# Where the output transposes find their PSUM bank, and when the sums of the heads' weights may start, in a two-layer graph-attention kernel

## The chip, the cores and the metric

One core of one Trainium2 chip. The metric is the device time of one execution in microseconds (us). Most executions agree within 0.3%. Faster or slower asks for 2%. A ratio is the mean time of one kernel's runs over the mean time of the other's runs of the same rounds, so it is not quite the ratio of the medians that are quoted beside it.

## The reference, cut to what matters

x is 128 graphs of 64 nodes with 512 features, all fp32. The layer is a norm, four attention heads, one more attention over the four heads' outputs, and a feed-forward with a residual and a second norm:

```python
h = relu(layernorm(x))
h = elu(gat_heads(h, adj, W_heads, a_heads))      # 4 heads, 512 -> 512 each
out = elu(gat_heads(h, adj, W_out, a_out))        # 2048 -> 512
y = relu(out @ w1 + b1) @ w2 + b2 + out
x + layernorm(y) * gamma + beta
```

## The kernel before

The 8192 rows are 64 tiles of 128, taken in 16 groups of four. Every large product is done with seven block products instead of eight (Strassen's way), so sums of weight blocks are formed once at the start by GpSimd and written to DRAM. TensorE works on one group's heads and output projection while the feed-forward of the group before and the attention of the group after are mixed in.

PSUM has eight banks here: a ring of six, tag "mm", and two auxiliary ones.

```python
ps = ctx.enter_context(tc.tile_pool(name="ps", bufs=6, space=bass.MemoryType.PSUM))

def bank(name):
    return ps.tile([P, 2, T], FP, tag="mm", name=name)

def aux(shape, name):
    return ps.tile(shape, FP, tag="aux", name=name, bufs=2)
```

Accumulators of the products (g1, g5, g6 of each unit) come from the ring. The attention of a tile takes two auxiliary banks for its first half and two of the ring for its second. ScalarE copies one bank of each pair out, VectorE the other:

```python
def task(j):                       # attend1, one tile
    ...
        if half == 1:
            banks = [bank(f"pz{nm}_{t}_{b}") for b in range(NB)]
        else:
            banks = [aux([P, 2, T], f"pz{nm}_{t}_{b}") for b in range(NB)]
        # ... eight matmuls for the two banks
    for nm, banks in done:
        for b in range(NB):
            ...
            if b == 0:
                nc.scalar.copy(dst, srcv)
            else:
                nc.vector.tensor_copy(dst, srcv)
```

For tiles 2 and 3 of a group the first half is "S1" (called pzS and zS in the profile), for tiles 0 and 1 it is "11" (pz, z). The feed-forward of the group before begins with four output transposes, one after each of these tasks, into an auxiliary bank as well:

```python
def transpose_out(j):
    ...
    pt = aux([P, KC, P], f"pto{g}_{j}")
    for k in range(KC):
        nc.tensor.transpose(pt[:, k, :], o[:, j, ts(k, P)], ident)
    nc.scalar.copy(OT[j // 2][:, :, ts(j % 2, P)], pt)
```

At the start, GpSimd does two things: a small power and a product for each tile's norm (n1rs, n1nb), which ScalarE's norm waits for, and the sums of weights. A tie keeps some sums behind the last tile's n1nb:

```python
def weight_sums(m, after=None):
    ...
    first = nc.gpsimd.tensor_tensor(s[0][:, 0], b12, b11, ALU.subtract)
    if after is not None:
        tc.add_manual_dep(first.ins, after.ins.name, ...)
    nc.gpsimd.tensor_tensor(s[0][:, 1], b22, s[0][:, 0], ALU.subtract)
    nc.gpsimd.tensor_tensor(s[1][:, 0], b22, b12, ALU.subtract)
    nc.gpsimd.tensor_tensor(s[1][:, 1], b21, s[0][:, 1], ALU.subtract)
    ...
for m in range(H):
    weight_sums(m, LAST["nb"] if m else None)
```

The names in the lines below: hn is the norm of a tile of x, pth and hT its transpose in PSUM and in SBUF. The start folds the weights of each head with its attention vector into wa: for heads 0, 1 and 3 VectorE does it (jk, out of the weights pw and of pab, the vector spread over all partitions by TensorE); for the third head, number 2, TensorE does it (pwt is the transposed weights, wT ScalarE's copy of them, aT the vectors, pwa the product). project_f (pf) multiplies hT by wa; L, U and R are made of pf; s1pe holds the first scores, R times L; s1e and s1A are steps of their softmax, s1pt its transpose. Then pz is attention times hn. g_a, g_b, g_c and g_d are accumulators of the heads' product, of the output projection (project2) and of the feed-forward's two products; zs_z holds sums of z for them. o is the layer's output, pto its transpose.

## Time and profile before

| | before |
|---|---|
| time, median of 3 runs | 2352.25 us (2352.14 to 2352.45) |
| span of the profiled run | 2349.7 us |
| TensorE busy, idle | 2281.3 us, 68.4 us |
| idle before output transposes | 26.3 us in 26 waits |
| first attention matmul (pz) | 54.16 us |

TensorE is the bound, so the idle 68.4 us are what a change of order can win; 26.3 of them repeat from group to group and most of the others lie in the first 54 us. The lines are in the prediction. In lines of single instructions the columns are start, duration, engine and line of the kernel, operation, output and inputs, and in square brackets the engine's idle time before it and what ended that.

### The profile page before, as it was taken

The page shows a single profiled execution, that of the slowest core. Times are in us where ns is not written, and L with a number is a line of the kernel's source. Part 1 is how long each engine was busy: PE and PEld are TensorE (multiplying, and loading weights), DVE is VectorE, ACT ScalarE, POOL GpSimd, SP SyncE. Part 2 cuts the span into 40 slices and gives each one's busy share as a digit, 9 for nine tenths or more (in the row PEclk, how much of TensorE's full clock was granted, in tenths as well). Part 3 has the DMA queues.
Part 4 walks back from the last instruction along what each step waited for, and adds up shares of the span by engine and source line. Part 5 has one row for each costly group of instructions (what it writes and reads, how often), then busy time and mean ns, then how long its engine had stood idle before and what let it go on. Part 6 is the DMA issues. An engine that isn't in the chain of part 4 may idle for free. (4 is left out here: it accounts for less than half of the span.)

```text
span 2349.7 us, 33387 instructions
## 1 busy us (share of the span) xinstructions
PE 2281.3 (97%) x11933; PEld 1921.8 (82%) x11933; DVE 1271.2 (54%) x2210; ACT 907.0 (39%) x1623; POOL 1031.2 (44%) x917
## 2 busy tenths in 40 slices
PE   6999999999999999999999999999999999999997
PEld 4878887888878888787888878888788887888885
DVE  5635465555646556464554655555465554744527
ACT  2534425253352533425244251533525344251512
POOL 5664444425344353443524444253443535533334
PEclk9999999999999999999999999999999999999999
DMA  8555464554645445464454645545454454645543
GB/s 287 158 183 193 129 182 132 156 160 131 182 127 173 134 143 178 127 181 129 145 173 129 182 132 156 160 130 180 129 172 136 142 178 124 181 123 158 169 148 104
DMA packets 259571, 366.40 MB, mean 156 GB/s; under 512 B 24232, under 2 KB 147144, under 8 KB 259408
## 3 DMA queue, kind: packets, MB, share of 16 engines
q1 hardware_dynamic: 252784, 343.31, 47.8%
q0 software_dynamic: 4512, 16.78, 1.9%
q10 hardware_dynamic: 2112, 4.19, 0.5%
q8 instruction: 96, 1.57, 0.3%
q14 instruction: 67, 0.55, 0.1%
HBM read 336.92 MB, written 27.26 MB: 155 GB/s over the span
## 5 line engine op out<-in xcount | busy, mean ns | idle before, releaser
L322 PE MATMUL g_b<-w,h 128*128 128x256 f32 x2560 | 592.5, 379 | 0.0
L322 PEld LDWEIGHTS g_b<-w,h 128*128 128x128 f32 x2560 | 481.4, 190 | 63.6 <-issue 0.9
L307 PE MATMUL g_a<-z,w 128*128 128x256 f32 x1520 | 360.9, 380 | 0.8 <-DVE g_a L597 0.7
L307 PE MATMUL g_a<-zs_z,w 128*128 128x256 f32 x1504 | 350.9, 381 | 0.0
L307 PEld LDWEIGHTS g_a<-zs_z,w 128*128 128x128 f32 x1504 | 282.1, 190 | 60.8 <-issue 24.3
L307 PEld LDWEIGHTS g_a<-z,w 128*128 128x128 f32 x1520 | 287.3, 190 | 45.0 <-DVE g_a L597 6.1
L601 POOL TENSOR_TENSOR hS<-hS,h 128x512 f32<-128x512 f32 x64 | 83.2, 1301 | 354.8 <-DVE hS L565 354.8
L322 PE MATMUL g_b<-w,hS 128*128 128x256 f32 x1024 | 238.5, 379 | 0.0
L563 ACT ACTIVATE exc<-g_a 128x512 f32<-128x512 f32 x256 | 152.1, 594 | 179.3 <-DVE g_a L597 106.0
L565 DVE SCALAR_TENSOR_TENSOR h<-exc,g_a 128x512 f32<-128x512 f32 x192 | 131.7, 686 | 156.0 <-ACT exc L564 156.0
L322 PEld LDWEIGHTS g_b<-w,hS 128*128 128x128 f32 x1024 | 192.1, 190 | 25.8 <-issue 1.0
L564 ACT ACTIVATE exc<-exc 128x512 f32<-128x512 f32 x256 | 161.5, 631 | 7.0
L631 POOL TENSOR_TENSOR h<-h,h 128x512 f32<-128x512 f32 x64 | 86.8, 1364 | 135.4 <-PE g_b L322 135.4
L631 POOL TENSOR_TENSOR h<-hS,h 128x512 f32<-128x512 f32 x64 | 81.1, 1269 | 142.5 <-PE g_b L322 142.5
L332 POOL TENSOR_TENSOR zs_z<-zS,z 128x512 f32<-128x512 f32 x63 | 89.0, 1414 | 122.4 <-PE g_a L307 118.4
L481 ACT COPY at<-s1pt 128x512 f32<-128x512 f32 x64 | 34.7, 588 | 279.8 <-PE s1pt L479 279.8
L773 POOL TENSOR_TENSOR xr<-xr,bs 128x512 f32<-128x512 f32 x64 | 95.7, 1500 | 72.8 <-DMA xr<-in_x_dram 40.6
L322 PE MATMUL g_d<-w,rt 128*128 128x256 f32 x512 | 121.5, 380 | 1.7 <-DVE o L765 1.0
L307 PE MATMUL g_c<-ot,w 128*128 128x256 f32 x512 | 122.5, 382 | 0.2 <-DVE ot L735 0.2
L307 PE MATMUL g_a<-zS,w 128*128 128x256 f32 x496 | 117.2, 379 | 0.0
L655 DVE SCALAR_TENSOR_TENSOR jf<-wh,ao 128x512 f32<-128x512 f32 x128 | 98.4, 806 | 32.5 <-ACT wh L637 32.3
L333 POOL TENSOR_TENSOR zs_z<-z,zs_z 128x512 f32<-128x512 f32 x63 | 85.2, 1354 | 62.3 <-PE g_a L307 39.6
(159 smaller groups left out, 3484.9 us busy)
## 6 DMA issues: line engine op xcount, KB each, us to landing
w<-tc SPq DMA_DIRECT2D x632, 256.0 KB, 2.7
w<-in_L_gnn_W_heads_dram SPq DMA_DIRECT2D x192, 256.0 KB, 3.2
w<-in_L_gnn_W_out_dram SPq DMA_DIRECT2D x192, 256.0 KB, 2.8
w<-in_L_gnn_w_dram SPq DMA_DIRECT2D x96, 256.0 KB, 2.7
x<-in_x_dram SPq DMA_DIRECT2D x64, 256.0 KB, 4.2
xr<-in_x_dram SPq DMA_DIRECT2D x128, 128.0 KB, 2.7
out_dram<-o SPq DMA_DIRECT2D x128, 128.0 KB, 2.4
tc<-pt POOLq DMA_DIRECT2D x20, 512.0 KB, 4.5
```

The lines of the kernel that those rows point to most:

```text
L307: LAST["pe"] = nc.tensor.matmul(bk[:, o, :], w[:, k, ts(o, P)], a[:, k, :], start=start and o == 0 and k == 0, stop=k == 1, skip_group_che ...
L322: LAST["pe"] = nc.tensor.matmul(bk[:, j, :], a[:, k, ts(j, P)], w[:, k, :], start=start and k == 0 and j == 0, stop=i == len(ms) - 1 and k ...
L332: eng.tensor_tensor(s2, s1, a11, ALU.subtract)
L333: eng.tensor_tensor(s4, a12, s2, ALU.subtract)
L481: nc.scalar.copy(AT[t].rearrange("p b h n -> p (b h) n"), pt)
L563: nc.scalar.activation(ex, src, AF.Relu, scale=-1.0)
L564: nc.scalar.activation(ex, ex, AF.Exp, scale=-1.0)
L565: nc.vector.scalar_tensor_tensor(dst, ex, -1.0, src, ALU.add, ALU.max)
L601: nc.gpsimd.tensor_tensor(dst, dst, H1["22"][:, h], ALU.add)
L631: nc.gpsimd.tensor_tensor(dst[:, h], x0[:, h], x1[:, h], ALU.subtract)
L655: nc.vector.scalar_tensor_tensor(junk, WH2[g][:, j], 1.0, ao[:, c, :], ALU.mult, ALU.mult, accum_out=f[:, c, j:j + 1],)
L773: nc.gpsimd.tensor_tensor(xr, xr, bs, ALU.add)
```

## The change

Its intent is to take away the two waits: the transposes use a bank of the ring, and every sum that needs only raw weights, of every head, waits for the last tile's first norm.

```diff
-        first = nc.gpsimd.tensor_tensor(s[0][:, 0], b12, b11, ALU.subtract)
-        if after is not None:
+        free = [nc.gpsimd.tensor_tensor(s[0][:, 0], b12, b11, ALU.subtract)]
+        nc.gpsimd.tensor_tensor(s[0][:, 1], b22, s[0][:, 0], ALU.subtract)
+        free.append(nc.gpsimd.tensor_tensor(s[1][:, 0], b22, b12, ALU.subtract))
+        for ins in free if after is not None else ():
             tc.add_manual_dep(
-                first.ins, after.ins.name,
+                ins.ins, after.ins.name,
                 ...
-        nc.gpsimd.tensor_tensor(s[0][:, 1], b22, s[0][:, 0], ALU.subtract)
-        nc.gpsimd.tensor_tensor(s[1][:, 0], b22, b12, ALU.subtract)
@@
-            pt = aux([P, KC, P], f"pto{g}_{j}")
+            pt = bank(f"pto{g}_{j}").rearrange("p a b -> p (a b)").rearrange("p (k n) -> p k n", k=KC)
@@
-        weight_sums(m, LAST["nb"] if m else None)
+        weight_sums(m, LAST["nb"])
```

## The prediction

> **What bounds the kernel now.** I read the page first, then all waits of TensorE, then busy times by stretch, then the order of time in one repeat of the steady state and in the first 55 us.
>
> ```profile
> PE 2281.3 (97%) x11933; PEld 1921.8 (82%) x11933; DVE 1271.2 (54%) x2210; ACT 907.0 (39%) x1623; POOL 1031.2 (44%) x917
> PEclk9999999999999999999999999999999999999999
> ```
>
> The span is 2349.7 us (2352.25 us is the timed median), so TensorE is idle for 2349.7 - 2281.3 = 68.4 us in all. No other engine is over 54%, and the clock is granted in full. A change that leaves the arithmetic alone, as this one does, can at most win those 68.4 us (2.9%). So the list of TensorE's waits is the list of what can be won:
>
> ```profile
> PE pto L725 <- ACT zS L551: 26.3, 26, 1.9
> PE pab L158 <- DMA ar<-in_L_gnn_a_heads_dram: 8.3, 1, 8.3
> PE s1pt L479 <- DVE s1A L442: 5.4, 1, 5.4
> PE pwa L193 <- ACT wT L191: 5.2, 1, 5.2
> ```
>
> The reader sees one wait that comes 26 times, and single ones of the start. The first is the output transposes waiting for a ScalarE copy of zS, which is no input of theirs: it only reads the PSUM bank that they are to be written to. The stretches show where it repeats:
>
> ```profile
> 380.00:520.00 140.00, 138.09 (x732) 116.78 (x731) 78.17 (x134) 54.71 (x99) 61.04 (x53) 1.00 0.50 152
> 520.00:660.00 140.00, 138.09 (x733) 116.78 (x732) 76.98 (x133) 54.64 (x99) 59.32 (x52) 1.00 0.51 154
> 2060.00:2200.00 140.00, 140.00 (x689) 119.34 (x688) 66.21 (x115) 50.84 (x91) 57.28 (x46) 1.00 0.51 153
> ```
>
> The second number is TensorE's busy time in 140 us. One repeat (a group of four tiles) is about 142.4 us long and loses 1.91 us; the stretch from 2060, where no first norms are left to do, loses nothing with the same banks. Inside a repeat:
>
> ```profile
> 397.40 0.69 DVE L553 COPY z<-pz 128x512 f32<-128x512 f32 x1 [0.24 <-PE pz L539]
> 397.41 0.81 ACT L366 ACTIVATE hn<-x,n1nb,n1rs 128x512 f32<-128x512 f32 x1
> 398.13 0.57 ACT L551 COPY zS<-pzS 128x512 f32<-128x512 f32 x1
> 398.59 0.59 ACT L551 COPY z<-pz 128x512 f32<-128x512 f32 x1
> 398.75 0.42 PEld L725 LDWEIGHTS pto<-ident,o 128*128 128x128 f32 x4 [1.89 <-ACT zS L551]
> 398.75 0.66 PE L725 MATMUL pto<-ident,o 128*128 128x128 f32 x4 [1.49 <-ACT zS L551]
> ```
>
> Both auxiliary banks hold pzS; ScalarE's part of the copy stands in its queue behind the norm of a later tile (hn); the transposes start 0.05 us after that copy ends (398.13 + 0.57 = 398.70). The fourth transposes of the group lose another 0.42 us in the same way, so 1.49 + 0.42 = 1.91 us. The first two of a group follow z11's copy and show no idle TensorE.
>
> The start, on GpSimd and ScalarE:
>
> ```profile
> 18.22 1.27 POOL L219 TENSOR_TENSOR pt<-pw,pt 128x512 f32<-128x512 f32 x1
> 19.43 1.31 POOL L222 DMA_DIRECT2D tc<-pt  x2
> 20.76 2.50 POOL L218 TENSOR_TENSOR pt<-pw 128x512 f32<-128x512 f32 x2
> 23.21 0.56 POOL L356 TENSOR_TENSOR n1rs<-n1ve,mhalf 128x1 f32<-128x1 f32 x1
> ...
> 24.17 1.69 ACT L366 ACTIVATE hn<-x,n1nb,n1rs 128x512 f32<-128x512 f32 x2 [8.34 <-POOL n1nb L364]
> 25.77 0.16 ACT L170 COPY aT<-pah 128x32 f32<-128x32 f32 x1
> 25.83 1.07 ACT L191 COPY wT<-pwt 128x512 f32<-128x512 f32 x2
> ```
>
> VectorE had the variances of tiles 2 and 3 at about 15.0 us, but GpSimd took up their small power operation (n1rs) only at 23.2, behind sums of weights that are needed much later. ScalarE stands for 8.34 us, and behind it in its queue the copies wT that TensorE's pwa waits for. The existing tie covers only the first sum of heads 1 to 3; L218, whose inputs are raw weights too, slips ahead of it.
>
> **What the Trainium skill says.** "Perfetto Trace Analysis", section "Identifying the Most-Contended Engine", warns that matmul occupancy is a poor measure of headroom and takes the weight loads' busy share instead. Here that is 82%, but in the repeats both are level from stretch to stretch, so I use idle time before named instructions, not the percentages. The same page, "Optimization Strategy", says that the same gap repeating on the saturated engine can mean too little PSUM for the next tile; this trace agrees: 26 gaps of one kind. "PSUM — Partial Sum Buffer", section "Specifications (TRN2)", gives 8 banks of 512 fp32 values; the ring of six and two auxiliary ones are all, and a transposed tile (128x512 fp32) fills one, so the change can only shift load between the two pools. That page's section "Engine vs sequencer instructions" says ScalarE's, VectorE's and GpSimd's queues are strict FIFO; both chains above are an urgent instruction behind an idle one, so the trace agrees.
>
> **The change part by part.** No operation is added or removed; banks and order change.
>
> *Part A, the bank.* A ring bank must be free when the third transposes of a group come. In the repeat above that is 397.3 us. Live in the ring are then: project2's first accumulator (begun at 381.1, read again for its second product some 20 us on) and the two pz banks of this tile (copied by 399.2). The other three were last read by 393 us: the two pz banks of the tile before (copies ended at 391.9 and 392.1) and the second output transpose (its copy ended at 392.5). One goes to the transposes, one to project2's next accumulator, one is left. At the fourth transposes (about 403 us in the new time) two accumulators and two pz banks are live, and two are free. The three or four further accumulators of the feed-forward come after that, as today. So I expect no new wait, and the two auxiliary banks, with 3.5 us of other matmuls between the third transposes and the next pzS, have time to be copied. Gain: 13 groups (1 to 13, the ones that still have norms) at some 2.0 us (1.91 in twelve of them, 1.49 + 1.87 = 3.36 in the last) = 12 x 1.91 + 3.36 = 26.3 us, just the line above. VectorE, GpSimd and the weight loads are tied to TensorE's progress and have slack (54%, 44%, DMA 0.5), so I let the gain run through whole, less 1 us for small new gaps: 25 us.
>
> *Part B, the sums.* Tied behind the last n1nb, the three sums that need raw weights cannot start before about 17 us: n1rs and n1nb of tiles 2 and 3 are 2 x (0.56 + 0.26) = 1.6 us after 15.0. So hn of tile 3 ends at about 18 instead of 25.9, 8 us earlier. TensorE cannot use it all: its transposes pwt of the third head end at 19.31 + 1.97 = 21.3 anyway, held by weights' landing and by VectorE's folds. So pwa starts at 21.3 instead of 26.47: 5.2 us, and the folds, project_f and the first scores follow in a chain of fixed lengths (VectorE's last folds start after a pab matmul that stands behind pwa). If the new order of instructions also puts pab earlier, up to 8. I take 6. The sums end on GpSimd at about 17 + 16 x 1.27 + 8 x 0.57 + 2 x 0.72 = 43 us instead of 41; head 0's are needed at about 55 and the written-back ones later, so that delay is hidden. From 60 us on TensorE is the bound (59.2 of 60 us busy), so the gain is kept to the end.
>
> Sum: 2352.25 - 25 - 6 = 2321 us, 1.3% less.
>
> **The rivals.** (1) *The wait moves into the ring.* If the bank given to the transposes or to the accumulator after them is one whose reader is late, the 1.9 us come back, or more: accumulators live 20 to 40 us. For it: project2 and the feed-forward together hold six accumulators at times. Against: they come after the last transposes, and in group 15 (2230 to 2244 us) four transposes pass with no idle time. Part A would then give 0 to 10 us, time 2335 to 2346; with a new wait of 3 us in each group it would be over 2360. (2) *ScalarE, not the bank, is the limit.* Its queue delays the copy of zS whatever bank the transposes use; the next pzS, or project1 through the sums of z, would then wait instead. For it: the copy is late because of a norm. Against: 3.5 us of cover, and ScalarE is busy only 39%. It would make the gain of A about half: 2333. (3) *The start is bound elsewhere.* DMA share is 0.87 in the first 54 us, and a first norm or the third head's weights may rest on a landing; B would then be 0 to 3 us: 2324 to 2327. (4) *The start does better*, if pab of head 3 moves ahead of pwa and VectorE's folds close up (they stand idle 8.1 + 4.8 us): B near 10, time 2317.
>
> **Range and chances.** Both parts in full with the better start give 2316; A at half and B at 3 give 2336. Range 2314 to 2337. Faster by over 2% needs 47 us of the 68.4 idle, of which A and B reach at most 37: 3%. Slower by over 2% needs a new wait of over 3 us in every group and nothing won: 3%. Within 2%: 94%.
>
> **What would show it.** Right: the wait of pto for zS is gone from TensorE's list, the stretches of 140 us show 140 busy, a repeat is 140.5 us long instead of 142.4, the idle time of TensorE is near 37 us. For B: n1rs of tile 2 at about 15 us, ScalarE's wait of 8.34 us gone, project1's first pz at about 48 instead of 54.16 us. Wrong: a new line of pto, g_b or g_c waiting for a copy of z or for an accumulator's reader (rival 1), of pzS or g_a waiting for ScalarE (rival 2), or pwa still at 26 us (rival 3).

## The result, and the profile after

The changed kernel takes 2320.33 us, median of 4 runs (2317.49 to 2320.77), against 2352.35 us of before in the same rounds: 32.0 us less. The ratio is 0.9861, with a 95% interval of 0.9844 to 0.9878: the same by the 2% rule, and clearly not by chance. The order of instructions on TensorE and ScalarE is exactly that of before; only GpSimd's order and a few of VectorE's small instructions at the start differ. So nearly the whole gain is waiting that went away: TensorE's idle time fell by 29.5 us, of the 31.0 us by which the two profiled spans differ.

TensorE's waits, all engines' instructions, longest first (the columns: who waited for whom, total us, times, longest us):

```profile
PE pab L158 <- DMA ar<-in_L_gnn_a_heads_dram: 8.2, 1, 8.2
PE s1pt L479 <- DVE s1A L442: 5.4, 1, 5.4
```

The line of 26.3 us is gone, and so is pwa's 5.2 us; nothing of their size stands in their place (the third longest wait is 2.8 us). The steady stretches of 140 us are full, from 240 to 1920 us (one of them; columns as in the prediction: stretch, its length, TensorE's busy time):

```profile
380.00:520.00 140.00, 140.00 (x742) 118.58 (x740) 78.33 (x134) 56.01 (x101) 60.22 (x53) 1.00 0.49 154
```

The same place in the repeat as the prediction showed of before, now in the changed kernel:

```profile
390.66 0.66 PE L725 MATMUL pto<-ident,o 128*128 128x128 f32 x4
...
390.88 0.81 ACT L366 ACTIVATE hn<-x,n1nb,n1rs 128x512 f32<-128x512 f32 x1
...
391.59 0.57 ACT L551 COPY zS<-pzS 128x512 f32<-128x512 f32 x1
```

ScalarE's copy of zS is as late as it was (it still follows the norm hn), but the transposes now run 0.9 us before it starts instead of 0.05 us after it ends. The first output transposes of successive groups started at 386.98 and 529.40 us before (a repeat of 142.42 us) and start at 380.44 and 520.82 us now (140.38 us).

The start, on GpSimd and ScalarE, in the changed kernel:

```profile
14.45 0.55 POOL L356 TENSOR_TENSOR n1rs<-n1ve,mhalf 128x1 f32<-128x1 f32 x1 [1.41 <-ACT hn L366]
...
16.31 1.28 POOL L210 TENSOR_TENSOR pt<-pw 128x512 f32<-128x512 f32 x1
...
15.39 1.68 ACT L366 ACTIVATE hn<-x,n1nb,n1rs 128x512 f32<-128x512 f32 x2 [0.32 <-POOL n1nb L364]
...
18.67 0.58 ACT L191 COPY wT<-pwt 128x512 f32<-128x512 f32 x1 [1.52 <-PE pwt L189]
```

The norm of tile 2 is served at 14.45 us instead of 23.21, and ScalarE's copies wT start at 18.67 instead of 25.83, now behind TensorE's pwt. TensorE's pwa starts at 20.99 instead of 26.47 us. The first pz, though, is at 49.61 instead of 54.16 us: of 5.5 us at pwa only 4.55 are left there. What lies between is the one place where the trace did not go as told; two of the instructions of that chain, in the changed kernel:

```profile
38.41 1.26 POOL L211 TENSOR_TENSOR pt<-pw,pt 128x512 f32<-128x512 f32 x1
...
38.91 1.32 DVE L399 TENSOR_TENSOR R<-U,headrow 128x512 f32<-128x512 f32 x1
...
40.37 1.99 PE L413 MATMUL s1pe<-R,L 64*64 64x256 f32 x16 [2.82 <-DVE n1ve L354]
```

and in the kernel before, where GpSimd had no sums left:

```profile
45.02 0.66 DVE L399 TENSOR_TENSOR R<-U,headrow 128x512 f32<-128x512 f32 x1
...
45.82 1.09 PE L413 MATMUL s1pe<-R,L 64*64 64x256 f32 x16 [2.16 <-DVE n1ve L354]
```

R took twice as long with a sum of weights running beside it, and the 16 score matmuls that wait for it took 1.99 us instead of 1.09 after a longer idle time. The granted clock of just these two stretches shows why the matmuls were slow (columns: stretch, its length, busy time of TensorE, of its weight loads, of VectorE, ScalarE and GpSimd, granted clock, DMA share, GB/s). First the changed kernel, then the kernel before:

```profile
40.37:42.36 1.99, 1.99 (x16) 0.86 (x16) 1.11 (x2) 0.00 (x0) 1.99 (x3) 0.50 0.98 290
```

```profile
45.82:46.91 1.09, 1.09 (x16) 0.57 (x16) 1.09 (x2) 0.00 (x0) 1.09 (x3) 0.99 0.68 239
```

Each trace also records when which clock was granted. It was full at 36.89 to 40.30 us in the changed kernel and at 43.48 to 46.90 in the kernel before, with half the clock after it (to 53.95 and 57.14 us). The score matmuls of the changed kernel started 0.07 us after that stretch had ended.

### The profile page after: what moved, and what is told of

It reads as the page before. It is cut to its first block, busy times and chain, and to the rows that moved or that the text cites. A ratio compares the mean times of both kernels' runs of the same rounds, so it can differ in the third digit from the quotient of the medians.

```text
span 2318.7 us, 33446 instructions
## 1 busy us (share of the span) xinstructions
PE 2279.8 (98%) x11933; PEld 1922.7 (83%) x11933; DVE 1272.2 (55%) x2210; ACT 905.5 (39%) x1623; POOL 1029.9 (44%) x917
```

## The experiments

**The theory**: (A) the transposes waited for nothing but a bank whose reader stood late in ScalarE's queue, another bank removes that whole, and nothing takes its place; (B) the start was held by sums of weights in front of the norms in GpSimd's queue. **The rivals**: the wait moves to the ring; ScalarE is the limit whatever the bank; the start is bound by something else. Runs e1 to e4 shared one chip and the runs of before (median 2352.01 us), as did e5 to e8 (2352.32 us) and e9 to e12 (2351.82 us).

### e1: the bank alone

Edit: the change's line of `pt = bank(...)` only. The order of instructions on every engine is that of before.

> Only the bank of the output transposes is changed; the sums keep their old tie. The order of instructions on every engine is that of the kernel before. My theory (the 26.3 us of waiting for the copy of zS is all bank, and nothing takes its place): 2325 to 2327 us, no wait of pto for zS left, 140.0 us busy in each steady stretch of 140. Rival 'ScalarE's queue is the limit': under half of it, 2338 or more, with new waits of pzS or g_a for ScalarE.

Measured: 2325.43 us (2324.28 to 2325.83), 26.6 us less, ratio 0.9886 (0.9872 to 0.9899). No wait of pto for zS is left and the steady stretches are 140.00 of 140 busy. Part A is as the theory has it; the rivals of part A would have left half or none of it.

### e2: the sums alone

Edit: the change without its line of `pt = bank(...)`.

> Only the sums are tied behind the last tile's norm; the transposes keep the auxiliary bank. My theory: the start is 4.5 us shorter as in the changed kernel's trace (first pz at 49.6 instead of 54.2 us) and TensorE's 26 us of waits stay: 2347 to 2348.5 us. If part of the 31 us comes from both together, this and the run with the bank alone do not add up to 31 to 32 us.

Measured: 2348.08 us (2347.95 to 2348.65), 3.9 us less, ratio 0.9984 (0.9971 to 0.9996); TensorE's 26.4 us of waiting for zS stay. Here R took 2.33 us beside the sums, and the first pz came at 49.88 us.

### e3: the old bank, but zS copied by VectorE

```diff
-                    if b == 0:
+                    if b == 0 and nm != "S1":
                         nc.scalar.copy(dst, srcv)
```

in the kernel before, with bank and tie as they were.

> The kernel before, with the bank and the tie as they were, but VectorE copies both banks of zS, so that neither stands in ScalarE's queue behind a norm. My theory (bank held by a copy that is late in ScalarE's queue): the third transposes' 1.49 us shrink to below 0.3, and the fourth's 0.42 too or nearly, so 2328 to 2334 us. If the cause were TensorE's transposes needing more banks as such, whoever empties them: the wait stays, 2350 us or more, now put down to VectorE.

Measured: 2326.01 us (2325.63 to 2326.4), 26.0 us less, ratio 0.9889 (0.9874 to 0.9904): a somewhat larger gain than expected and nearly what the other bank gives. (The order of TensorE's instructions differs in places from that of before.) In this run's trace the norm is still in ScalarE's queue, and it does not matter:

```profile
395.60 1.29 DVE L553 COPY zS<-pzS 128x512 f32<-128x512 f32 x2 [1.09 <-PE pzS L539]
...
396.36 0.66 PE L725 MATMUL pto<-ident,o 128*128 128x128 f32 x4
396.59 0.81 ACT L366 ACTIVATE hn<-x,n1nb,n1rs 128x512 f32<-128x512 f32 x1
```

One of the two auxiliary banks was free in time, and the transposes start with no idle TensorE. So two auxiliary banks were enough, and the wait was the late reader's: a bank that is freed in time and another bank that is free are two cures of one wait.

### e4: the change once more

> The changed kernel once more, on the chip and in the rounds of the single parts. 2318 to 2321 us; the parts alone should add up to this within 1.5 us.

Measured: 2318.78 us (2317.71 to 2320.49), 33.2 us less, ratio 0.9859 (0.9846 to 0.9873). The parts alone add to 26.6 + 3.9 = 30.5 us, 2.7 us short; I had allowed 1.5, so this expectation failed. The traces show where: in the profiled run of e4 the first eight pwa matmuls took 0.95 us, in those of e2 and of the first run of the changed kernel 1.70 to 1.71 us, with the same instructions in the same order. e4's first pz came at 47.54 us, theirs at 49.88 and 49.61. So the opening itself runs in one of two paces, some 2 to 3 us apart (project_f, before anything collides, starts at 31.84 us in e4, at 34.70 in e2 and at 35.41 in the changed kernel's first run), and a median of four runs probably mixes them (2317.49 us is the lowest and 2320.77 us the highest of the eight runs of the changed kernel). The clock records tell the two apart. In e4 the full clock was granted from 19.78 to 23.19 us, over the first sixteen pwa matmuls (0.95 us for eight), and half from there to 33.43 us, where the other sixteen took 3.58 us; in e7 below, the other fast opening, full from 20.48 to 23.89. In e2 and in the changed kernel's first run the record has no entry before 35.43 and 36.89 us (the view prints 1.00 for a stretch without an entry), and all their pwa went at the pace of e4's half clock, so I take it that they ran at half. Why the full clock is granted early in some runs stays open. In what follows I compare the openings of like pace, by their traces.

### e5: head 0's sums left untied

```diff
-        weight_sums(m, LAST["nb"])
+        weight_sums(m, LAST["nb"] if m else None)
```

in the changed kernel.

> The changed kernel (transposes in the ring), but head 0's sums stay untied; for heads 1 to 3 all three sums of raw weights are tied. GpSimd then does head 0's four sums and two transfer issues before n1rs of tile 2, which I put at 19.5 us (23.2 before, 14.5 in the changed kernel). pwa at about 22.9 us (26.5 before, 21.0 changed), so 1.5 to 2.5 us slower than the changed kernel of these rounds: about 2321. If the tie of head 0 is what matters, 4 us slower (2323 or more).

Measured: 2320.91 us (2320.34 to 2321.68), ratio to before 0.9868 (0.9851 to 0.9884). The places are as expected: n1rs of tile 2 at 19.44 us, pwa at 22.71. Yet the first pz is at 50.33 us, only 0.7 us after the changed kernel's, though pwa is 1.7 later: the sums end earlier, R took 0.66 us, and the score matmuls, 1.20 us long, met the full clock for most of their time.

### e6: only the first sum of each head tied

```diff
-        for ins in free if after is not None else ():
+        for ins in free[:1] if after is not None else ():
```

in the changed kernel.

> The changed kernel, but of each head only the first sum is tied, head 0 included (the half of the tie that the kernel before lacked for head 0). The four other raw sums still slip ahead: n1rs of tile 2 at about 18 us. The transposes of the third head end at 21 us anyway, so pwa at about 21.4 and the time within 1 us of the changed kernel. If every us of GpSimd counts, 3 us slower.

Measured: 2324.35 us (2324.27 to 2324.8), ratio 0.9882 (0.9867 to 0.9896): nearly all of part B is lost (the first pz is at 53.79 us, against 54.16 before), and the expectation failed. GpSimd's queue shows why:

```profile
21.54 1.27 POOL L212 TENSOR_TENSOR pt<-pw 128x512 f32<-128x512 f32 x1 [3.96 <-DMA pw<-in_L_gnn_W_heads_dram]
22.77 0.54 POOL L356 TENSOR_TENSOR n1rs<-n1ve,mhalf 128x1 f32<-128x1 f32 x1
```

The untied sum of head 3 needs weights that landed only at 21.5 us. It is first in a queue that is served in order, so the norm stands 3.96 us behind a transfer that is none of its business. I had counted the work in front of the norm, and not its waits.

### e7: head 3's sums behind the first softmax

```diff
-    for m in range(H):
+    for m in range(3):
         weight_sums(m, LAST["nb"])
@@
     softmax_end = LAST["A"]
+    for m in range(3, H):
+        weight_sums(m, softmax_end)
```

in the changed kernel.

> The changed kernel, but head 3's sums wait for the end of the first softmax, so that GpSimd is idle beside VectorE's first scores. Theory from the runs so far: the tied sums run 2 us later while VectorE's chain runs 5.5 us earlier, they now overlap, and VectorE's instructions with two SBUF inputs (R at 1.3 to 2.3 us instead of 0.66, two of the softmax at 2 us instead of 0.69) are held up by them. Expect all of these back at 0.7 us, and 1 to 2.5 us less than the changed kernel: about 2317. Rival: their length has another cause (data not there yet); then they stay long and the time stays at 2318.5 to 2320.

Measured: 2317.04 us (2314.97 to 2319.45), ratio 0.985 (0.9836 to 0.9865). R took 0.66 us, the softmax's instructions 0.66 to 0.69, and the score matmuls 1.09 us. Its profiled run opened in the faster pace (pwa 0.97 us), so it is to be held against e4's: first pz at 44.90 instead of 47.54 us, 2.6 us. In e4 it was two of the softmax's instructions that had been long, beside the same sums:

```profile
38.36 2.09 DVE L431 SCALAR_TENSOR_TENSOR s1e<-s1e 128x512 f32<-128x512 f32 x1
...
41.21 1.97 DVE L434 TENSOR_TENSOR s1e<-s1e,s1mx 128x512 f32<-128x512 f32 x1
```

The reduction between them kept its 0.69 us, but no sum ran beside it (GpSimd was at n1rs, from 39.86 to 41.40 us), so it is no test.

### e8: pab of head 3 ahead of the third head's fold

```diff
+    ab[3] = spread_a(3)
     fold_pe(2, aT)
@@
-    fold_dve(3, spread_a(3))
+    fold_dve(3, ab[3])
```

in the changed kernel.

> The changed kernel, with the two matmuls pab of head 3 issued ahead of the third head's fold on TensorE. Tests what the prediction left as its fourth rival: the gain of the sums is limited because pab of head 3 stands behind pwa. VectorE's folds should then run without the two gaps (3.5 and 4.8 us in the changed kernel), and TensorE's pwa chain should have a third buffer for its copies. Expect the first pz 3 to 6 us earlier than in the changed kernel, time 2313 to 2317. If instead the transposes pwt, now waiting for a bank behind VectorE's first folds, set the start, no gain or a loss.

Measured: 2320.72 us (2320.18 to 2321.26), ratio 0.9866 (0.985 to 0.988): no gain. The edit did what it was for: project_f starts at 32.32 us instead of 35.41. Then comes R, here VectorE's and GpSimd's lines of the same time:

```profile
35.83 4.68 DVE L399 TENSOR_TENSOR R<-U,headrow 128x512 f32<-128x512 f32 x1
...
36.25 1.27 POOL L210 TENSOR_TENSOR pt<-pw 128x512 f32<-128x512 f32 x1
37.48 1.26 POOL L212 TENSOR_TENSOR pt<-pw 128x512 f32<-128x512 f32 x1
38.70 1.26 POOL L211 TENSOR_TENSOR pt<-pw,pt 128x512 f32<-128x512 f32 x1
```

R, 0.66 us of work, ends at 40.51 us, 0.55 us after the third of three sums in a row. The score matmuls start at 40.66 us, against 40.37 in the changed kernel: all 3 us are given back. (They also took 1.99 us, at a granted clock of 0.50.) This is the clearest sight of what also cost part B its last part.

The Trainium skill has the mechanism: "SBUF — State Buffer", section "Who interferes with whom", says that a VectorE instruction with two SBUF inputs contends with a GpSimd instruction that reads SBUF, and one with a single SBUF input does not. The traces agree: R and the two softmax instructions above, with two inputs in SBUF, went from 0.66 to as much as 4.68 us and from 0.69 to 2.09 and 1.97 us. In all six cases in the openings where such an instruction of R or of the softmax met a sum (the changed kernel, e2, e4 twice, e6, e8), it ended 0.55 or 0.56 us after the last sum that it met. The statistics of x, with one input, took 1.28 us for two beside sums (changed kernel, 36.94 to 38.22 us) as without (before, 42.59 to 43.87), and the mask's addition, whose other input is in PSUM, kept 0.69 us beside a sum (e4, 37.64 to 38.33).

### e9: a ring of five

`bufs=6` of the pool set to 5 in the changed kernel; one bank of PSUM is unused.

> The changed kernel with a ring of five banks instead of six (one bank of PSUM unused). By the count in the prediction the transposes find exactly one free bank even then, but project2 and the feed-forward hold six accumulators at once a little later. Expect waits of TensorE for accumulators' readers in every group, 1 to 3 us each in 14 groups: 2333 to 2360 us. If the ring has a bank to spare all the time, 2319 to 2322 us.

Measured: 2323.26 us (2322.41 to 2325.04), ratio 0.9879 (0.9864 to 0.9893). The expectation failed: the steady stretches are full (139.98 to 140.00 of 140 us busy). What it loses lies at the start, where the first pz is at 50.98 us, and in single waits of 0.9 to 1.9 us (after the longest, near 1946 us, the granted clock was half for 3.41 us). The order of TensorE's instructions differs in places (the order is fitted to the banks when the kernel is built), so this is not the same program with a bank less; but rival 1, a ring too tight for the transposes, has nothing left.

### e10: a ring of five and three auxiliary banks

The transposes stay in auxiliary banks, of which there are three.

> The changed kernel, but the transposes stay in the auxiliary banks, of which there are now three, and the ring has five. The wait of the third transposes for zS should be gone as in the change (a third bank is free), so what this loses against the changed kernel is the ring of five's: within 3 us of the run with five in the ring and two auxiliary ones. If it is at 2318 to 2322, a bank moved from the ring to the auxiliary ones would have done as well as the change.

Measured: 2320.83 us (2317.99 to 2321.79), ratio 0.9865 (0.9851 to 0.988). The steady stretches are full here too, so a bank moved between the pools does for part A what the change does. Its start is slower (first pz at 52.07 us): project_f's matmuls wait four times for VectorE's folds, 2.5 us in all. That the ring has a bank less there would explain it, but no run separates the two.

### e11: e7 and e8 together

> Both of the last round's edits: pab of head 3 ahead of pwa, and head 3's sums behind the first softmax. In the run with pab alone, R took 4.68 us beside the sums of head 3, and ate what was won. Expect R at 0.7 to 1.2 us, the first pz at 45 to 46.5 us, time 2314 to 2317. If R stays above 2 us, its length does not come from the sums.

Measured: 2317.36 us (2316.79 to 2318.04), ratio 0.9853 (0.9837 to 0.987). R is at 0.66 us and the first pz at 45.52 us, in the slower pace (pwa 1.71 to 1.87 us), against 49.61 us in the changed kernel at that pace: 4.1 us, of which 3.8 show in the time of the two profiled runs (2316.79 against 2320.63 us). R and the clock of the score matmuls (1.09 us here, 1.99 there) account for some 1.6 of the 4.1 us, so by this estimate pab gave some 2.5. So rival 4 of the prediction, pab behind pwa, was real, and hidden by R; the medians of e7 and e11, which mix the paces, do not show it. e7 and e11 have the lowest medians of all; 1 to 3 us under the changed kernel is far inside the 2% rule and partly inside the mix of the two paces.

### e12: heads 2 and 3 later

As e11, with `range(2)` and `range(2, H)`.

> The same with the sums of heads 2 and 3 behind the first softmax. R at 0.66 us; time 2313 to 2317, equal to or up to 1 us below the run with head 3 alone. If head 2's sums then come too late for its pieces (the load queue would wait for the written-back sums at 60 to 80 us), slower: 2320 or more, with TensorE waiting for w.

Measured: 2325.92 us (2325.27 to 2327.68), ratio 0.989 (0.9875 to 0.9905): slower than expected, and not for the reason that I had named. R is fine (0.66 us), but TensorE has a new wait of 6.34 us. Its chain, from three engines of this run:

```profile
64.71 0.81 ACT L366 ACTIVATE hn<-x,n1nb,n1rs 128x512 f32<-128x512 f32 x1 [4.51 <-POOL n1nb L364]
65.43 0.56 ACT L551 COPY zS<-pzS 128x512 f32<-128x512 f32 x1
...
66.03 2.16 DVE L332 TENSOR_TENSOR zs_z<-zS,z 128x512 f32<-128x512 f32 x1 [4.26 <-ACT zS L551]
...
68.25 3.78 PE L307 MATMUL g_a<-zs_z,pt 128*128 128x256 f32 x8 [6.34 <-DVE zs_z L332]
```

GpSimd does the two heads' sums until 62.5 us and only then the n1rs of the next norms; ScalarE's norm waits for it, the copy of zS stands behind that norm, VectorE's sum of z waits for the copy (and then runs 2.16 us beside GpSimd), and TensorE for the sum. During that wait the granted clock fell to 0.50 (65.28 to 72.11 us), so these eight matmuls took 3.78 us and the next eight of g_a, from 72.84 us on, 1.89. It is part B's fault and part A's fault in one chain. The sums have a window: not before the norms of one group, not beside the first scores, and not before the norms of the next.

## Why the prediction was right

The time foretold was 2321 us and the time measured 2320.33, in a range of 2314 to 2337. By its steps:

- **The bound.** Right. The gain is idle TensorE that went away: 68.4 us before, 2318.7 - 2279.8 = 38.9 us after (foretold: near 37).
- **Part A, 25 us.** Right, a little short. From the first output transposes of group 1 to those of group 14 it took 2097.42 - 244.56 = 1852.86 us before and takes 2065.96 - 240.07 = 1825.89 us now: 27.0 us over 13 repeats; e1 gave 26.6 us. The 1 us taken off for new gaps did not come, and the idle time in the list says slightly too little: the ends of matmuls are modelled and overlap the start of the next, so a wait of 1.49 + 0.42 us in the list shortened the repeat by 2.05 us.
- **No new wait in the ring.** Right, with more room than counted: even five banks keep the steady state full (e9). The only waits that grew after the start are for VectorE, by 0.5 us (g_d) and 1.2 us (g_c).
- **ScalarE is not the limit behind the bank (rival 2).** Right. Nothing that waits for ScalarE grew; e3 shows that the same 26 us come back when ScalarE's copy is taken out of its queue.
- **Part B, 6 us.** The mechanism was right: norm at about 15 us (14.45), ScalarE's wait of 8.34 us gone, pwa limited by pwt and not by the norm (20.99 us, foretold 21.3). The size was not: 3.9 us alone (e2), 4.5 us in the trace of the changed kernel, both with the slower opening. (With e4's faster one the first pz came 6.6 us earlier than before: 47.54 us.) The term that was mis-sized is the one that read "so that delay is hidden". The sums do end at about 43 us (the last transfer is issued at 42.36 to 43.5), and nobody waits for their results; but VectorE's chain now runs 5.5 to 6 us earlier, so sums and chain overlap, and R and the scores after it pay. In the changed kernel U, VectorE's instruction before R, starts 6.1 us earlier than before (38.43 against 44.54), the end of R 5.45 (40.23 against 45.68), and the first read of the scores 4.56 (42.38 against 46.94): 0.66 us lost in R and 0.9 in the score matmuls.
- **Why the score matmuls were slow.** The clock records answer it, and the prediction, which read "the clock is granted in full" from slices of 59 us, had not seen it. In eight runs the full clock was granted over all or most of the sixteen, and they took 1.09 to 1.42 us; in the changed kernel, e2, e3 and e8 the clock stood at half, and they took 1.98 to 1.99 us; in e9 and e10 they took the same, before the first entry of the record (52.52 and 53.58 us). In the changed kernel it needed R's delay to miss the full clock, which ended at 40.30 us: with R at 0.66 us the scores would have started near 39.7 and met the full clock for some 0.6 us (an estimate, from 40.37 - 0.66). But e3 lost the same 0.9 us with R at 0.66 us, and the place of the stretch varies from run to run: before, e1 and e3 open alike (project_f at 41.06, 40.88 and 40.87 us), and their full clock came at 43.48, 42.85 and 41.45 us. "TensorE: Matmul & The Clock Gate", section "What's actually happening", says that TensorE falls to half its clock after an idle window of some 3.4 us, and that the window runs free of the kernel. The length agrees: the stretches of full clock before or at the scores last 3.41 us. What decides their place is not shown here.
- **The start does better (rival 4).** Not in the changed kernel, as its order on TensorE stayed; e11 shows that it could.

The total came closer than its parts: A was 2 us too low, and B, with the slower opening, 1.5 to 2 us too high. That the two errors cancel is luck.

## What to carry to other kernels

A wait for a PSUM bank is a wait for the bank's reader: look at what stands before that reader in its engine's queue, and cure it with another bank or with another reader, whichever is free. On an in-order queue a tie must cover every instruction that can slip in front of the urgent one, those that would wait for a transfer above all. Before calling moved work hidden, ask what it will now run beside: sums that nobody waits for still doubled VectorE's instructions with two SBUF inputs, and once made one seven times as long. And before two single openings are compared, read the granted clock of the very stretch: the same eight matmuls took 0.95 us or 1.70 by it.

## What the Trainium skill lacked or had wrong

- "SBUF — State Buffer", "Who interferes with whom", has the contention right, but says that issue order decides who blocks. Here R started at 35.83 us, 0.42 us before the first of three sums in a row, and ended at 40.51 us, after the third (e8); an instruction of the softmax that started under one sum (37.42 to 38.68 us) also waited through the next (38.64 to 39.89 us), and ended at 40.45 (e4). By these records VectorE's instruction lost to GpSimd's even where its start was recorded first, and to a row of instructions, not to one. (Spans on GpSimd are rough in these profiles; the row of sums is not in doubt.)
- "TensorE: Matmul & The Clock Gate", "What's actually happening", gives an idle window as what brings back half the clock. In e4 the full clock of 19.78 to 23.19 us was followed by half although the profile counts TensorE busy for all of those 3.41 us, with 27 matmuls, 16 of them the small ones of pwa; in the kernel before, after 43.48 to 46.90 us with 1.26 us busy. So half the clock also followed windows that were not idle. The page also says that the warm-up varies from run to run, and this agrees: the first full clock came at 19.78 us in one run of the changed kernel and at 36.89 us in another.
- "Perfetto Trace Analysis", "Optimization Strategy", says that a repeating gap can mean too little PSUM. e3 is a case where the same gap closed with the same two banks (26.0 us of 26.6): a repeating gap before a PSUM write can as well mean a late reader.
